# Moving some row gathers of a recommendation kernel from GpSimd to SyncE

## The chip, the cores and the metric

The kernel runs on one core of one Trainium2 chip. The metric is the device time in microseconds (us) of one execution. The time before is 13297.63 us, the median of three runs (13260.15 to 13308.35). The profile is of one execution, which took 13172.43 us.

## What is computed

For each of 16384 requests there are 69 item ids and one label id. Each id picks a row of 96 floats from a table of 100001 rows. A small network (attention) turns each item row, together with the label's row, into one weight; the weighted rows are summed in 10 groups of fields; and three layers on top (200, 80, 1) turn the 10 sums and the label's row into one number.

```python
u  = emb[batch_user]                     # [B, 69, 96]   B = 16384
ql = emb[batch_label[:, 0]]              # [B, 96]
q  = broadcast(ql[:, None, :], u.shape)
z  = concatenate([q, u, q - u, q * u], axis=-1)
h  = _dice(z @ W1 + b1, a1, EPS_DICE)    # 64 wide; _dice needs a sigmoid
h  = h @ W2 + b2                         # 16 wide
att = h @ W3 + b3                        # 1 wide
pre = where((batch_user < ITEM_NUM)[..., None], u * att, 0.0)
pooled = einsum('gf,bfe->bge', window, pre).reshape(B, G * E)   # G = 10 groups
x = concatenate([pooled, ql], axis=-1)
h = _dice(_bn_eval(x @ Wf1 + bf1, EPS_BN), af1, EPS_DICE)       # 200
h = _dice(_bn_eval(h @ Wf2 + bf2, EPS_BN), af2, EPS_DICE)       # 80
return h @ Wf3 + bf3                                            # 1
```

The work is thus 16384 x 70 = 1.15 million rows of 384 B, picked at random from memory, and a modest amount of matrix work in float32 on each.

## The kernel before

The requests are worked on in 32 blocks of 512. The items of a block are cut into 69 chunks of 512 rows: 64 "main" chunks of 8 requests x 64 fields, and 5 "tail" chunks with one of the last five fields of all 512 requests. Two chunks make a pair, and there are 1104 pairs. One tile of 128 rows is fetched by one gather of GpSimd (an indirect DMA with 128 ids, a list that lies in the on-chip memory): 276 gathers per block for the items, and 4 for the labels.

```python
def gather(table, dst, index):
    nc.gpsimd.indirect_dma_start(out=dst, out_offset=None, in_=table,
                                 in_offset=bass.IndirectOffsetOnAxis(ap=index, axis=0))

def head_gather(n):                       # the 4 x 128 label rows of block n
    q = bpool.tile([P, NQ, E], F32, tag="q", name=f"q{n}")       # 2 buffers
    for k in range(NQ):
        gather(emb, q[:, k, :], ids[n][:, NT + k : NT + k + 1])
    return q

def fetch(i, between=None):               # pair i: 8 gathers, 8 transpositions
    u = upool.tile([P, 8, E], F32, tag="u", name=f"u{i}")        # 14 buffers
    ...
    for j in range(2):
        ...
        n, k = chunk(2 * i + j)
        ptr = ps_tr.tile([E, 512], F32, tag="tr", name=f"ptr{i}_{j}")
        for t in range(4):
            gather(rows, u[:, 4 * j + t, :], ids[n][:, 4 * k + t : 4 * k + t + 1])
            nc.tensor.transpose(ptr[:, t * P : (t + 1) * P], u[:, 4 * j + t, :], ident)
        # VectorE: quT = ptr * q; ScalarE: uT = copy of ptr
        ...
```

After the transposition a pair goes through these steps, each some pairs later: `hidden` (the first layer on TensorE, tile ph, two steps after the fetch; ScalarE and VectorE make y of it), `attend_rows` and `spread` (the attention weight of each row, tiles prow, patt and rw), and `pool`, which multiplies the rows with their weights and sums them by group, reading u once more:

```python
def pool(i):
    u, rw = us.pop(i), rws.pop(i)
    ...
    pa = ps_acc.tile([E, 2, NS, G], F32, tag="acc", name=f"acc{i}")   # 1 buffer
    for j, n, k in todo:                  # main chunks only
        for t in range(4):
            nc.tensor.matmul(pa[:, j, 2 * t : 2 * t + 2, :]..., u[:, 4 * j + t, :], rw[:, t, j, :], ...)
    ...                                   # VectorE: pooled <- pa
```

The order of all this is a plan with one step for each pair, written out by hand. `POOL_LAG` is 8:

```python
for i in range(close):
    if i >= POOL_LAG:
        at(i, pool_of(i - POOL_LAG))
    if i >= 3 and (i - 3) % 4 == 3:
        at(i, rows_of(i - 6, 4))
    ...
    if i >= 2:
        at(i, hidden_of(i - 2))
    at(i, fetch_of(i))
...
for n in range(NBLK):
    first, end = n * NCH // 2, ((n + 1) * NCH - 1) // 2
    if n > 0:
        if n % NIDS == 1:
            at(first - 20, lambda n=n: load_ids(n))        # ids of 4 blocks, by SyncE
        at(first - 14, lambda n=n: qs.__setitem__(n, head_gather(n)))
        at(first - 11, lambda n=n: head_turn(n, qs.pop(n)))  # transposes the label rows
        at(first - 9, lambda n=n: head_rows(n))
```

At the end of the last block the top layers are done by quarters of 128 requests, in between the last pairs (`quarter[r][s]` is step s of quarter r: 0 to 3 and 4 to 7 the two halves of the first layer, 8 the second, 9 the third):

```python
d = NPAIR
at(d, pool_of(c + 4), hidden_of(c + 7), pool_of(c + 5), *quarter[2][0:4], rows_of(c + 6, 2), *quarter[2][4:8])
at(d, quarter[2][8], spread_of(c + 6, 2), quarter[2][9], quarter[3][0])
at(d, pool_of(c + 6), pool_of(c + 7), lambda: store(B // P - 1), *quarter[3][1:])
```

The weights come in two packs, `near` (first layer) by SyncE and `far` (top layers) by ScalarE's queue.

Of the kernel before, what the change touches and what calls it, by code (L numbers as in the profile page):

```python
# [32 lines left out]
F32 = mybir.dt.float32  # L33
I32 = mybir.dt.int32
# [4 lines left out]
P = 128  # L39
B, F, E, G = 16384, 69, 96, 10  # L40
ITEM_NUM = 100000
H1, H2 = 64, 16
D1, D2 = 200, 80
DH = D1 // 2

BLK = 512
NBLK = B // BLK
# [5 lines left out]
NQ = BLK // P  # L53
NT = NCH * 4
# [5 lines left out]

POOL_LAG = 8

NIDS = 4

EARLY = 20
# [49 lines left out]
def rec_kernel(  # L115
    ctx: ExitStack,
    tc: tile.TileContext,
    idx0: bass.AP,
    idx: bass.AP,
    emb: bass.AP,  # L120
    rows: bass.AP,
    near: bass.AP,
# [3 lines left out]
    nc = tc.nc  # L126
# [4 lines left out]
    tpool = ctx.enter_context(tc.tile_pool(name="tpool", bufs=4))  # L131
    ypool = ctx.enter_context(tc.tile_pool(name="ypool", bufs=6))
    rpool = ctx.enter_context(tc.tile_pool(name="rpool", bufs=2))
    bpool = ctx.enter_context(tc.tile_pool(name="bpool", bufs=2))
    xpool = ctx.enter_context(tc.tile_pool(name="xpool", bufs=1))

    def by_field(ap):

        return ap.rearrange("e (s o) -> e s o", o=1).to_broadcast([ap.shape[0], NS, FM])

    ids = {0: const.tile([P, NCOL], I32, name="ids0")}
    nc.sync.dma_start(out=ids[0], in_=idx0)

    def load_ids(n):

        t = ipool.tile([P, NIDS, NCOL], I32, tag="ids", name=f"ids{n}")
        nc.sync.dma_start(out=t.rearrange("p b n -> p (b n)"), in_=idx[(n - 1) // NIDS])
        for k in range(NIDS):
            ids[n + k] = t[:, k, :]
# [2 lines left out]
    wn = const.tile([P, NEAR.width], F32, name="wn")  # L152
    nc.sync.dma_start(out=wn, in_=near)
    wf = const.tile([P, FAR.width], F32, name="wf")
    nc.scalar.dma_start(out=wf, in_=far)

    ident = const.tile([P, P], F32, name="ident")
    make_identity(nc, ident)
# [25 lines left out]
    for i in range(2):  # L184
        t = const.tile([E + 1, BLK], F32, name=f"qT{i}")
# [55 lines left out]
    ps_h = ctx.enter_context(tc.tile_pool(name="ps_h", bufs=2, space=PSUM))  # L241
    ps_x = ctx.enter_context(tc.tile_pool(name="ps_x", bufs=2, space=PSUM))
    ps_acc = ctx.enter_context(tc.tile_pool(name="ps_acc", bufs=1, space=PSUM))
    ps_m = ctx.enter_context(tc.tile_pool(name="ps_m", bufs=1, space=PSUM))
# [11 lines left out]
    def gather(table, dst, index):  # L256
        nc.gpsimd.indirect_dma_start(  # L257
            out=dst,
            out_offset=None,
            in_=table,  # L260
            in_offset=bass.IndirectOffsetOnAxis(ap=index, axis=0),
        )
# [5 lines left out]
            k = NMAIN + k - EARLY if k < EARLY + NTAIL else k - NTAIL  # L268
        return n, k

    def head_gather(n):

        q = bpool.tile([P, NQ, E], F32, tag="q", name=f"q{n}")
        for k in range(NQ):
            gather(emb, q[:, k, :], ids[n][:, NT + k : NT + k + 1])
        return q

    def head_turn(n, q):
        pq = ps_x.tile([E, BLK], F32, tag="x", name=f"pq{n}")
        for k in range(NQ):  # L280
            nc.tensor.transpose(pq[:, k * P : (k + 1) * P], q[:, k, :], ident)
        nc.vector.tensor_copy(qTs[n % 2][0:E, 0:BLK], pq)
# [18 lines left out]
    def fetch(i, between=None):  # L301

        u = upool.tile([P, 8, E], F32, tag="u", name=f"u{i}")
        uT = []
        quT = tpool.tile([E, 2, 512], F32, tag="quT", name=f"quT{i}")
        for j in range(2):
            if j == 1 and between:
                between()
            n, k = chunk(2 * i + j)
            ptr = ps_tr.tile([E, 512], F32, tag="tr", name=f"ptr{i}_{j}")  # L310
            for t in range(4):
                gather(rows, u[:, 4 * j + t, :], ids[n][:, 4 * k + t : 4 * k + t + 1])
                nc.tensor.transpose(ptr[:, t * P : (t + 1) * P], u[:, 4 * j + t, :], ident)  # L313
            q = qTs[n % 2][0:E]
            if k < NMAIN:
                nc.vector.tensor_tensor(  # L316
                    quT[:, j, :].rearrange("e (s f) -> e s f", f=FM),
                    ptr.rearrange("e (s f) -> e s f", f=FM),
                    by_field(q[:, k * NS : (k + 1) * NS]),
                    ALU.mult,  # L320
                )
            else:
                nc.vector.tensor_tensor(quT[:, j, :], ptr, q[:, 0:BLK], ALU.mult)
            uT.append(room(k))
            nc.scalar.copy(uT[j][0:E], ptr)  # L325
        return u, uT, quT

    def hidden(i, uT, quT):

# [57 lines left out]
    def pool(i):  # L387

        u, rw = us.pop(i), rws.pop(i)
        todo = [(j, *chunk(2 * i + j)) for j in range(2)]  # L390
        todo = [(j, n, k) for j, n, k in todo if k < NMAIN]
        if not todo:
            return
        pa = ps_acc.tile([E, 2, NS, G], F32, tag="acc", name=f"acc{i}")
        for j, n, k in todo:
            for t in range(4):
                nc.tensor.matmul(  # L397
                    pa[:, j, 2 * t : 2 * t + 2, :].rearrange("e n g -> e (n g)"),
                    u[:, 4 * j + t, :],
                    rw[:, t, j, :],  # L400
                    start=True,
                    stop=True,
                )
        if len(todo) == 2:
            _, n, k = todo[0]
            nc.vector.tensor_copy(  # L406
                pooled[n][:, :, k * NS : (k + 2) * NS].rearrange("e g s -> e s g"),
                pa.rearrange("e j s g -> e (j s) g"),
            )
        else:  # L410
            j, n, k = todo[0]
            nc.vector.tensor_copy(
                pooled[n][:, :, k * NS : (k + 1) * NS].rearrange("e g s -> e s g"), pa[:, j]
            )
# [10 lines left out]
    def top1(n, cols, h, part, p1):  # L425

        if part == 0:
            p1 = ps_m.tile([DH, BLK], F32, tag="m", name=f"p1_{n}_{h}_{cols.start}")[:, cols]
        for k in range(part * KTOP // 4, (part + 1) * KTOP // 4):
            if k < NTAIL:  # L430
                w, x = V[:, k], pres[n][:, k, cols]
            elif k == NTAIL:
                w, x = wf1[:, G], qTs[n % 2][0:E, cols]
            else:
                w, x = wf1[:, k - NTAIL - 1], pooled[n][:, k - NTAIL - 1, cols]
            nc.tensor.matmul(p1, w[:, h * DH : (h + 1) * DH], x, start=(k == 0), stop=(k == KTOP - 1))  # L436
        if part < 3:
            return p1
        g1 = xpool.tile([DH, BLK], F32, tag="g1", name=f"g1_{n}_{h}_{cols.start}")[:, cols]
        dice(x1s[n][:, h, cols], g1, p1, bf1c[h], dice1[h])  # L440
# [17 lines left out]
    def store(n):  # L458

        p4 = ps_x.tile([n, P], F32, tag="x", name="p4")  # L460
        nc.tensor.transpose(p4, res[:, 0:n], ident)
        r = ypool.tile([P, 512], F32, tag="y", name="r")[0:n, 0:P]
        nc.vector.tensor_copy(r, p4)
        nc.sync.dma_start(out=out[0 : n * P].rearrange("(m p) o -> m (p o)", p=P), in_=r)
# [6 lines left out]
        nc.vector.tensor_scalar(r, p3, bf3c[0:1], None, ALU.add)  # L471
        nc.sync.dma_start(out=out[B - P :].rearrange("p o -> o p"), in_=r)

    pooled, pres, x1s, x2s, qs, us, hs, ys, bands, rws, p1s = ({} for _ in range(11))

    def top_steps(n, cols):

# [14 lines left out]
    def rows_of(b, n):  # L492
        return lambda: attend_rows(b, n)

    def spread_of(b, n):
        return lambda: spread(b, n)

    def pool_of(k):
        return lambda: pool(k)

    def hidden_of(k):
        return lambda: ys.__setitem__(k, hidden(k, *hs[k]))
# [25 lines left out]
    def at(step, *work):  # L528
        plan.setdefault(step, []).extend(work)
# [15 lines left out]
    c = close  # L545
# [9 lines left out]
    for n in range(NBLK):  # L555
        first, end = n * NCH // 2, ((n + 1) * NCH - 1) // 2
        if n > 0:
            if n % NIDS == 1:
                at(first - 20, lambda n=n: load_ids(n))
            at(first - 14, lambda n=n: qs.__setitem__(n, head_gather(n)))  # L560
            at(first - 11, lambda n=n: head_turn(n, qs.pop(n)))
            at(first - 9, lambda n=n: head_rows(n))
        if n < NBLK - 2:
            for s, work in enumerate(top_steps(n, slice(0, BLK))):
                at(end + POOL_LAG + 4 + s, work)
        elif n == NBLK - 2:
            for s, work in enumerate(top_steps(n, slice(0, BLK))):
                at(end + POOL_LAG + s // 2, work)
# [3 lines left out]
    quarter = [top_steps(NBLK - 1, slice(r * P, (r + 1) * P)) for r in range(NQ)]  # L572
# [2 lines left out]
        at(c + s // 3, quarter[1][s])  # L575

    d = NPAIR
    at(d, pool_of(c + 4), hidden_of(c + 7), pool_of(c + 5), *quarter[2][0:4], rows_of(c + 6, 2), *quarter[2][4:8])
    at(d, quarter[2][8], spread_of(c + 6, 2), quarter[2][9], quarter[3][0])
    at(d, pool_of(c + 6), pool_of(c + 7), lambda: store(B // P - 1), *quarter[3][1:])  # L580

    with tc.manual_schedule():
        qs[0] = head_gather(0)
        head_turn(0, qs.pop(0))
        head_rows(0)
        ones()
        for i in range(NPAIR + 1):
            for work in plan.pop(i, []):
                work()
# [63 lines left out]
```

## Time and profile before

| engine or queue | busy, us | share of the span | instructions |
|---|---|---|---|
| TensorE, matmuls | 8747.3 | 66% | 41797 |
| TensorE, weight loads (beside matmuls) | 4554.2 | 35% | 41797 |
| VectorE | 3029.0 | 23% | 5325 |
| ScalarE | 3167.1 | 24% | 4969 |
| GpSimd | 8455.0 | 64% | 8966 |
| DMA queue of the gathers, of 16 engines | | 16.0% | 286720 packets |

The span is 13170.6 us. How to read it: the busy time of an engine leaves out what its sequencer does between two instructions, so an engine can be full at less than 100%. TensorE's clock is granted by a throttle; its mean was 0.732 of full speed. In the tables of groups a row names the line, the engine, the operation and "tile written <- tiles read", then the count, the busy time in all, the mean of one in ns, and the idle time just before these instructions with what ended most of it. In the timeline a row has its start, its duration (both us), the engine, the line, and in square brackets the idle time before it with what ended it. "issue" means that the profile shows nothing that the engine waited for.

The gathers begin at 7.04 us and the last one starts at 13051.49 us; the last instruction ends at 13170.6 us.

### The profile page before, as it was taken

What the parts mean: (1) busy time and instruction counts of PE and PEld (TensorE: products, weight loads), DVE (VectorE), ACT (ScalarE), POOL (GpSimd) and SP (SyncE); (2) the same over time, 40 slices, a digit from 0 to 9 for tenths busy, and PEclk for the clock granted to TensorE, in tenths of its full rate; (3) what the DMA queues carried; (4) which work ended last, traced back from release to release, by engine and by line L of the source; (5) the groups of instructions that cost most, each with busy time, mean ns of one, the idle gap of its engine ahead of it and who ended that gap; (6) DMA issues with size and microseconds to landing.
All of it is one profiled execution on the core that took longest, in us unless ns stands there. A gap on an engine that the chain in (4) does not pass through costs nothing.

```text
span 13170.6 us, 108463 instructions
## 1 busy us (share of the span) xinstructions
PE 8747.3 (66%) x41797; PEld 4554.2 (35%) x41797; DVE 3029.0 (23%) x5325; ACT 3167.1 (24%) x4969; POOL 8455.0 (64%) x8966
## 2 busy tenths in 40 slices
PE   3666666667666676666766667666666666676667
PEld 2333333333333333333333333333333333333334
DVE  2222222222222222222222222222222222222222
ACT  1222222222222222222222222222222222222222
POOL 6666666666666666666666666666666666666664
PEclk6777777777777777767777777777777777777777
DMA  1111111111111111111111111111111111111111
GB/s 40 35 35 34 34 34 37 34 36 34 34 36 34 35 35 35 37 34 34 35 34 37 33 35 34 34 36 35 35 35 33 36 34 35 35 35 35 35 34 22
DMA packets 288946, 454.19 MB, mean 34 GB/s; under 512 B 143538, under 2 KB 143922, under 8 KB 288306
## 3 DMA queue, kind: packets, MB, share of 16 engines
q0 software_dynamic: 286720, 440.98, 16.0%
q8 instruction: 335, 5.49, 0.2%
q1 hardware_dynamic: 1570, 5.04, 0.1%
q14 instruction: 177, 1.45, 0.0%
q10 hardware_dynamic: 144, 1.24, 0.0%
HBM read 446.61 MB, written 0.07 MB: 34 GB/s over the span
## 4 chain that ended last, share of the span: by engine, by line
PE 54%; issue 20%; another core or an unknown queue 16%; POOL 4%; ACT 3%; DVE 3%; DMA 1%; DVEq 0%; POOLq 0%
PE acc L397 11%; PE ptr L313 9%; PE ph L338 9%; PE ph L342 8%; PE p L436 7%; PE prow L353 4%; POOL u L257 3%; PE patt L370 1%; DVE quT L316 1%; PE pa L362 1%; ACT uT L325 1%; ACT y L345 1%; PE ph L335 1%; PE pc L290 1%
## 5 line engine op out<-in xcount | busy, mean ns | idle before, releaser
L257 POOL DMA_INDIRECT u<-in_rows,ids x8832 | 8333.2, 944 | 4552.4 <-issue 2367.4
L397 PE MATMUL acc<-rw,u 128*96 128x20 f32 x16384 | 1922.1, 260 | 1844.3 <-issue 1436.2
L397 PEld LDWEIGHTS acc<-rw,u 128*96 128x96 f32 x16384 | 1911.1, 197 | 2083.9 <-issue 1613.1
L313 PE MATMUL ptr<-ident,u 128*96 128x128 f32 x8832 | 1594.5, 316 | 1395.4 <-issue 1099.1
L325 ACT COPY uT<-ptr 96x512 f32<-96x512 f32 x2208 | 1283.3, 581 | 3091.3 <-DVE quT L316 1905.9
L313 PEld LDWEIGHTS ptr<-ident,u 128*96 128x96 f32 x8832 | 1079.1, 143 | 2732.2 <-issue 2182.7
L344 ACT ACTIVATE y<-ph 128x512 f32<-128x512 f32 x1104 | 659.3, 597 | 5104.0 <-remote 2661.7
L342 PE MATMUL ph<-quT,wn 96*64 96x512 f32 x4416 | 1693.6, 744 | 165.9 <-issue 158.6
L346 DVE TENSOR_TENSOR y<-ph,y 128x512 f32<-128x512 f32 x1104 | 763.5, 692 | 4287.1 <-ACT y L345 2399.0
L338 PE MATMUL ph<-uT,A 128*64 128x512 f32 x4096 | 1631.8, 800 | 145.8 <-issue 142.8
L316 DVE TENSOR_TENSOR quT<-ptr,qT 96x512 f32<-96x512 f32 x2048 | 1337.6, 680 | 1419.3 <-remote 892.2
L406 DVE COPY pooled<-acc 96x160 f32<-96x160 f32 x1008 | 429.6, 426 | 3547.6 <-remote 2121.3
L345 ACT ACTIVATE y<-y,wn,na1c 128x512 f32<-128x512 f32 x1104 | 897.8, 813 | 36.7
L342 PEld LDWEIGHTS ph<-quT,wn 96*64 96x64 f32 x4416 | 449.0, 172 | 1201.8 <-issue 1199.3
L353 PE MATMUL prow<-y,v 128*32 128x512 f32 x2208 | 629.5, 787 | 254.1 <-issue 150.2
L436 PE MATMUL p<-pooled,wf 96*100 96x512 f32 (+1 forms) x1400 | 616.5, 583 | 0.0
L338 PEld LDWEIGHTS ph<-uT,A 128*64 128x64 f32 x4096 | 280.6, 162 | 683.7 <-issue 664.9
L355 ACT COPY row<-prow 128x512 f32<-128x512 f32 (+1 forms) x277 | 161.8, 584 | 1421.8 <-remote 878.8
L370 PE MATMUL patt<-ident,row 128*128 128x128 f32 x1108 | 241.2, 338 | 277.6 <-issue 203.7
L436 PE MATMUL p<-pre,V 96*100 96x512 f32 (+1 forms) x700 | 372.7, 665 | 40.6 <-issue 25.8
L436 PEld LDWEIGHTS p<-pooled,wf 96*100 96x100 f32 x1400 | 233.7, 179 | 291.7 <-issue 291.6
L375 DVE SCALAR_TENSOR_TENSOR rw<-patt,bb,wn 128x320 f32<-128x320 f32 x554 | 273.4, 534 | 142.2 <-remote 64.3
(66 smaller groups left out, 2139.8 us busy)
## 6 DMA issues: line engine op xcount, KB each, us to landing
u<-in_rows,ids POOLq DMA_INDIRECT x8832
ids<-in_idx SPq DMA_DIRECT2D x8, 560.0 KB
q<-in_emb,ids POOLq DMA_INDIRECT x128
wf<-in_far ACTq DMA_DIRECT2D x1, 1209.0 KB
wn<-in_near SPq DMA_DIRECT2D x1, 236.0 KB
ids<-in_idx SPq DMA_DIRECT2D x1, 140.0 KB
out<-r SPq DMA_DIRECT2D x1, 63.5 KB
out<-r SPq DMA_DIRECT2D x1, 0.5 KB
```

The costliest lines, as they stand in the source:

```text
L257: nc.gpsimd.indirect_dma_start(out=dst, out_offset=None, in_=table, in_offset=bass.IndirectOffsetOnAxis(ap=index, axis=0),)
L313: nc.tensor.transpose(ptr[:, t * P : (t + 1) * P], u[:, 4 * j + t, :], ident)
L316: nc.vector.tensor_tensor(quT[:, j, :].rearrange("e (s f) -> e s f", f=FM), ptr.rearrange("e (s f) -> e s f", f=FM), by_field(q[:, k * NS ...
L325: nc.scalar.copy(uT[j][0:E], ptr)
L338: nc.tensor.matmul(p, As[n % 2][:, k // 4, :], uT[j], start=True, stop=False)
L342: nc.tensor.matmul(p, Wp, quT[:, j, :], start=False, stop=True)
L344: nc.scalar.activation(y, ph, AF.Sigmoid, scale=S_DICE)
L345: nc.scalar.activation(y, y, AF.Identity, bias=a1c, scale=na1c)
L346: nc.vector.tensor_mul(y, ph, y)
L353: nc.tensor.matmul(pr[32 * k : 32 * (k + 1), :], v2, ys[b + k], start=True, stop=True)
L397: nc.tensor.matmul(pa[:, j, 2 * t : 2 * t + 2, :].rearrange("e n g -> e (n g)"), u[:, 4 * j + t, :], rw[:, t, j, :], start=True, stop=True,)
L436: nc.tensor.matmul(p1, w[:, h * DH : (h + 1) * DH], x, start=(k == 0), stop=(k == KTOP - 1))
```

## The change

Three things change. First, in each block but the first, the four tiles of label rows and one tile of item rows (the first of chunk 8, `SOLO = 32` counted in tiles) are no longer gathered by GpSimd. SyncE loads the 640 ids of the block (20 x 32), reads 32 of them at a time into registers, and issues one copy for each row. This is spread over 20 steps of the plan, from 32 to 13 pairs before the block. It is meant to take work off GpSimd, which issues all the gathers. Second, the pack `far` is loaded by SyncE behind the first ids and `near`, so that these need not share the DMA engines with it. Third, the work at the end of the last block is ordered anew, and in the last two quarters the second half of the first layer gets an accumulation buffer of another pool, so that less of it waits.

```diff
+NLD = 32
+PARTS = P // NLD
+SOLO = 4 * 8
...
+    spool = ctx.enter_context(tc.tile_pool(name="spool", bufs=2))
...
-    nc.scalar.dma_start(out=wf, in_=far)
+    nc.sync.dma_start(out=wf, in_=far)
...
-    def head_gather(n):
-        q = bpool.tile([P, NQ, E], F32, tag="q", name=f"q{n}")
+    def first_head():
+        q = bpool.tile([P, NQ, E], F32, tag="q", name="q0")
         for k in range(NQ):
-            gather(emb, q[:, k, :], ids[n][:, NT + k : NT + k + 1])
+            gather(emb, q[:, k, :], ids[0][:, NT + k : NT + k + 1])
         return q
+
+    def load_solo(n):
+        t = spool.tile([(NQ + 1) * PARTS, NLD], I32, tag="sid", name=f"sid{n}")
+        nc.sync.dma_start(out=t, in_=solo[n])
+        return t
+
+    def fetch_rows(table, dst, index):
+        _, at = nc.values_load_multi_w_load_instructions(
+            index, engines=[mybir.EngineType.SP], min_val=0, max_val=ITEM_NUM, ...)
+        for i, row in enumerate(at):
+            nc.sync.dma_start(out=dst[i : i + 1, :], in_=table[bass.ds(row, 1), :])
+
+    def solo_part(n, part):
+        if part == 0:
+            qs[n] = bpool.tile([P, NQ, E], F32, tag="q", name=f"q{n}")
+        if part == NQ * PARTS:
+            solos[n] = spool.tile([P, E], F32, tag="solo", name=f"solo{n}")
+        k, m = divmod(part, PARTS)
+        table, dst = (emb, qs[n][:, k, :]) if k < NQ else (rows, solos[n])
+        fetch_rows(table, dst[m * NLD : (m + 1) * NLD, :], sids[n][part : part + 1, :])
...
             for t in range(4):
-                gather(rows, u[:, 4 * j + t, :], ids[n][:, 4 * k + t : 4 * k + t + 1])
-                nc.tensor.transpose(ptr[:, t * P : (t + 1) * P], u[:, 4 * j + t, :], ident)
+                if n > 0 and 4 * k + t == SOLO:
+                    tiles.append(solos.pop(n))
+                else:
+                    tiles.append(u[:, 4 * j + t, :])
+                    gather(rows, tiles[-1], ids[n][:, 4 * k + t : 4 * k + t + 1])
+                nc.tensor.transpose(ptr[:, t * P : (t + 1) * P], tiles[-1], ident)
...
-            p1 = ps_m.tile([DH, BLK], F32, tag="m", ...)[:, cols]
+            banks, tag = (ps_h, "h") if n == NBLK - 1 and cols.start >= BLK // 2 and h == 1 else (ps_m, "m")
+            p1 = banks.tile([DH, BLK], F32, tag=tag, ...)[:, cols]
...
-            at(first - 14, lambda n=n: qs.__setitem__(n, head_gather(n)))
+            at(first - 33, lambda n=n: sids.__setitem__(n, load_solo(n)))
+            for part in range((NQ + 1) * PARTS):
+                at(first - 32 + part, lambda n=n, part=part: solo_part(n, part))
...
-    at(d, pool_of(c + 4), hidden_of(c + 7), pool_of(c + 5), *quarter[2][0:4], rows_of(c + 6, 2), *quarter[2][4:8])
-    at(d, quarter[2][8], spread_of(c + 6, 2), quarter[2][9], quarter[3][0])
-    at(d, pool_of(c + 6), pool_of(c + 7), lambda: store(B // P - 1), *quarter[3][1:])
+    at(d, pool_of(c + 4), hidden_of(c + 7), pool_of(c + 5), *quarter[2][0:4], rows_of(c + 6, 2), quarter[2][4])
+    at(d, spread_of(c + 6, 2), *quarter[2][5:8], pool_of(c + 6), quarter[2][8], pool_of(c + 7))
+    at(d, quarter[2][9], quarter[3][0], lambda: store(B // P - 1), *quarter[3][1:])
```

More of the change, by code (lines that the diff above doesn't have):

```diff
@@ L119, in rec_kernel @@
     idx: bass.AP,
+    solo: bass.AP,
     emb: bass.AP,
@@ L269, in chunk @@
         return n, k
-    def head_gather(n):
-        q = bpool.tile([P, NQ, E], F32, tag="q", name=f"q{n}")
+    def first_head():
+        q = bpool.tile([P, NQ, E], F32, tag="q", name="q0")
         for k in range(NQ):
-            gather(emb, q[:, k, :], ids[n][:, NT + k : NT + k + 1])
+            gather(emb, q[:, k, :], ids[0][:, NT + k : NT + k + 1])
         return q
+    def load_solo(n):
[4 more added lines that the diff above has]
+        _, at = nc.values_load_multi_w_load_instructions(
+            index,
+            engines=[mybir.EngineType.SP],
+            min_val=0,
+            max_val=ITEM_NUM,
+            skip_runtime_bounds_check_because="ids are rows of the table",
+        )
+        for i, row in enumerate(at):
[8 more added lines that the diff above has]
+        fetch_rows(table, dst[m * NLD : (m + 1) * NLD, :], sids[n][part : part + 1, :])
     def head_turn(n, q):
@@ L303, in fetch @@
         u = upool.tile([P, 8, E], F32, tag="u", name=f"u{i}")
-        uT = []
+        uT, tiles = [], []
         quT = tpool.tile([E, 2, 512], F32, tag="quT", name=f"quT{i}")
@@ L325, in fetch @@
             nc.scalar.copy(uT[j][0:E], ptr)
-        return u, uT, quT
+        return tiles, uT, quT
     def hidden(i, uT, quT):
@@ L398, in pool @@
                     pa[:, j, 2 * t : 2 * t + 2, :].rearrange("e n g -> e (n g)"),
-                    u[:, 4 * j + t, :],
+                    u[4 * j + t],
                     rw[:, t, j, :],
@@ L427, in top1 @@
         if part == 0:
-            p1 = ps_m.tile([DH, BLK], F32, tag="m", name=f"p1_{n}_{h}_{cols.start}")[:, cols]
+            banks, tag = (ps_h, "h") if n == NBLK - 1 and cols.start >= BLK // 2 and h == 1 else (ps_m, "m")
+            p1 = banks.tile([DH, BLK], F32, tag=tag, name=f"p1_{n}_{h}_{cols.start}")[:, cols]
         for k in range(part * KTOP // 4, (part + 1) * KTOP // 4):
@@ L472, in top3_last @@
         nc.sync.dma_start(out=out[B - P :].rearrange("p o -> o p"), in_=r)
-    pooled, pres, x1s, x2s, qs, us, hs, ys, bands, rws, p1s = ({} for _ in range(11))
+    pooled, pres, x1s, x2s, qs, us, hs, ys, bands, rws, p1s, sids, solos = ({} for _ in range(13))
     def top_steps(n, cols):
@@ L577, in rec_kernel @@
     d = NPAIR
-    at(d, pool_of(c + 4), hidden_of(c + 7), pool_of(c + 5), *quarter[2][0:4], rows_of(c + 6, 2), *quarter[2][4:8])
-    at(d, quarter[2][8], spread_of(c + 6, 2), quarter[2][9], quarter[3][0])
-    at(d, pool_of(c + 6), pool_of(c + 7), lambda: store(B // P - 1), *quarter[3][1:])
+    at(d, pool_of(c + 4), hidden_of(c + 7), pool_of(c + 5), *quarter[2][0:4], rows_of(c + 6, 2), quarter[2][4])
+    at(d, spread_of(c + 6, 2), *quarter[2][5:8], pool_of(c + 6), quarter[2][8], pool_of(c + 7))
+    at(d, quarter[2][9], quarter[3][0], lambda: store(B // P - 1), *quarter[3][1:])
     with tc.manual_schedule():
-        qs[0] = head_gather(0)
-        head_turn(0, qs.pop(0))
+        head_turn(0, first_head())
         head_rows(0)
@@ L617 @@
         "idx": groups.transpose(0, 2, 1, 3).reshape(-1, P, NIDS * NCOL),
+        "solo": np.concatenate([x["batch_label"].reshape(NBLK, BLK), main[:, :, SOLO]], axis=1).reshape(NBLK, -1, NLD),
         "emb": x["emb"],
```

## The prediction

> **What bounds the kernel now.** I read the page's first part, then its groups of instructions, the table of waits, and last the timeline of one stretch. The first part looks as if no engine were full; the group of the gathers is the largest of all:
>
> ```profile
> PE 8747.3 (66%) x41797; PEld 4554.2 (35%) x41797; DVE 3029.0 (23%) x5325; ACT 3167.1 (24%) x4969; POOL 8455.0 (64%) x8966
> ...
> L257 POOL DMA_INDIRECT u<-in_rows,ids x8832 | 8333.2, 944 | 4552.4 <-issue 2367.4
> ```
>
> One gather is 944 ns busy, and behind nearly each stands a gap of 0.30 us in which the engine waits for nothing (7751 such gaps make 2367.4 us). In the timeline gathers that follow each other start 1.248 us apart (7 of them from 6199.22 to 6207.95). With the 128 gathers of the label rows there are 8960: 8960 x 1.248 = 11,182 us in which GpSimd can do nothing else. They run from 7.0 to 13,052 us, so GpSimd stands still for 13,045 - 11,182 = 1,863 us. The table of waits says for whom:
>
> ```profile
> POOL u L257 <- issue: 2367.4, 7751, 1.5
> POOL u L257 <- remote: 978.9, 318, 7.4
> ...
> POOL u L257 <- PE acc L397: 462.2, 107, 39.8
> POOL u L257 <- PE ptr L313: 434.0, 201, 5.7
> ...
> PE ptr L313 <- DMA u<-in_rows,ids: 63.9, 66, 2.4
> ```
>
> The reader is to see two opposite sides. GpSimd waits for TensorE: a tile u is free only when the pooling matmul (acc) of its pair of chunks is done, 8 pairs after its transposition, and there are 14 buffers; so GpSimd is about 6 pairs (48 gathers) ahead when it stops. TensorE hardly waits for a gather: 63.9 us in the whole run. By these two alone TensorE is the bound, and a cheaper GpSimd would bring nothing.
>
> But TensorE is 66% busy, and its idle time is "issue", which no semaphore explains. The timeline shows what that is, here TensorE and then GpSimd in one stretch:
>
> ```profile
> 6174.88 0.30 PE L313 MATMUL ptr<-ident,u 128*96 128x128 f32 x1 [0.44 <-issue]
> 6194.28 2.11 PE L397 MATMUL acc<-rw,u 128*96 128x20 f32 x12 [19.10 <-issue]
> 6197.99 0.19 PE L397 MATMUL acc<-rw,u 128*96 128x20 f32 x1 [1.60 <-issue]
> ...
> 6206.40 0.19 PE L397 MATMUL acc<-rw,u 128*96 128x20 f32 x1 [2.62 <-issue]
> 6209.19 1.01 PE L353 MATMUL prow<-y,v 128*32 128x512 f32 x1 [2.60 <-issue]
> 6211.99 3.82 PE L353 MATMUL prow<-y,v 128*32 128x512 f32 x5 [1.79 <-issue]
> ```
>
> ```profile
> 6207.95 0.94 POOL L257 DMA_INDIRECT u<-in_rows,ids  x1 [0.30 <-issue]
> 6216.18 0.94 POOL L257 DMA_INDIRECT u<-in_rows,ids  x1 [7.29 <-PE prow L353]
> ```
>
> Matmuls that take 0.09 us elsewhere come 2.8 us apart here, for nearly 40 us, while GpSimd gathers without a stop; GpSimd starts its last gather at 6207.95, runs into full buffers, and some 3 us later TensorE is fast again. The same order stands at 6086-6090, 6109-6113 and 6041-6044. I take it that **the slow stretches of TensorE last as long as GpSimd keeps gathering**: GpSimd gathers for about two pairs (16 x 1.248 = 20 us), stops for some 3 us, and TensorE does its two pairs in the 12 us behind that stop. The pace is then GpSimd's time plus its stops, although the waits say the opposite. This is an inference from the order of events; I can't name the mechanism, and it is the weakest step here.
>
> **What the Trainium skill says.** *Perfetto Trace Analysis*, section "DMA Optimizations", says that where descriptor generation is the limit, spreading DMAs over the engines that can issue them may help: the idea of the change. Here GpSimd is full with issuing while the DMA queue's share is 16.0% of 16 engines, which agrees. *DMA: Bandwidth & Descriptors*, section "Why a DMA increments its semaphore by 16 and not by 1", says that a transfer of one partition runs on one DMA engine, the lowest. The trace agrees as to the number: the SyncE queue has 1570 packets; ten loads of 128 rows with 16 completions make 1440, and the two stores of 127 and 1 rows leave 130 = 127 + 1 + one completion each. So all rows of SyncE go through one DMA engine of 16. The same page, "Latency and other measured facts", gives a floor of about 600 ns for loading registers from a tensor, and *Runtime: NRT & Kernel Launch*, "Instruction fetch mechanics", about 200 ns a register. No run here shows either yet.
>
> **The change part by part.**
>
> 1. Removed from GpSimd: in each of 31 blocks 4 label gathers and one tile's gather, 31 x 5 = 155 gathers x 1.248 = **193 us**. If the number and length of GpSimd's stops stay, the end comes 193 us earlier (1.45%). If TensorE sets its own pace, nothing comes of it.
>
> 2. Added to SyncE: 31 x 640 = 19,840 row copies of 384 B, each with one small register instruction ahead, and 31 x 20 = 620 register loads of 32 ids. The nearest thing in the trace is the last store, of one row:
>
> ```profile
> 13168.46 0.26 SPq L472 DMA_DIRECT2D out<-r  x1
> ```
>
> 0.26 us, and I add 0.12 us for the register instruction and the gaps (issues at the start stand about 0.05 us apart beyond their own time): an estimate of 0.38 us a row, 640 x 0.38 = 243 us per block. The 20 loads are 12 us by the floor of 600 ns and 128 us by 200 ns a register, by the skill's figures. SyncE needs an estimated **255 to 371 us per block**; a block lasts 13,045 / 32 = 408 us. It fits, with 9 to 37% to spare. Rows begin 32 pairs ahead of their block and the tiles have two buffers, so a short lag is absorbed. With 70 us for loads a row may cost up to (408 - 70) / 640 = 0.53 us before SyncE becomes the bound. Each copy also waits for the one eight before it; at the 2 us or so that a gather takes from issue to landing that is 0.25 us a row, below the issue time.
>
> 3. Added to TensorE: the transpositions of label rows and of the extra tile wait for eight DMA semaphores instead of few, 31 x 16 = 496 waits of 0.05 us (a semaphore instruction of TensorE lasts 51 ns in the trace), at most 25 us, most of it in its idle time: +10 us.
>
> 4. The weights of the top layers (1209 KB) now go behind the first ids and the near weights on one queue. Before, the first ids landed at about 7.0 us with that load beside them. At most -3 us; I put -2.
>
> 5. The end: the pooling matmuls of the last two pairs come one at a time between other matmuls, and the last quarter's second half has a PSUM bank of its own. What it can take away is seen here:
>
> ```profile
> 13151.25 0.42 DVE L406 COPY pooled<-acc 96x160 f32<-96x160 f32 x1 [3.99 <-PE acc L397]
> 13151.73 2.75 PE L397 MATMUL acc<-rw,u 128*96 128x20 f32 x16 [0.52 <-DVE pooled L406]
> ```
>
> Gaps of 0.5, 1.0 and 1.4 us on TensorE and some matmuls at half clock (2.75 instead of 1.53 us): -5 us. The drain of the last six pairs, from 13,052 to 13,170 us, stays.
>
> Sum: -193 + 10 - 2 - 5 = -190, that is 13,108 us. As one of the rivals may hold in part, I put the middle at 13,130.
>
> **The rivals.** (a) *TensorE is the bound by itself.* For it: the waits above. Against: its slow stretches end with GpSimd's stops, also where these come late. Then only parts 3 to 5 remain: about 13,300 us. (b) *SyncE becomes the bound.* For it: 19,840 issues in a row, estimated from a single store whose address is fixed; a register address may cost more. At 0.65 us a row and 70 us of loads a block would take 486 us, in all some 15,000 us. It is steep: nothing up to 0.53 us, and then 20 us a block for each further 0.03 us. (c) *The rows disturb what the stops restore.* If TensorE needs a pause of all DMA traffic and not of GpSimd alone, a steady stream of rows takes the pauses away; 13,400 us or more. The traffic is little (640 rows of 35,840 per block), so I hold it for possible, not likely. (d) *The slow stretches shorten more than in proportion*, as fewer gathers fall between two stops: below 13,030.
>
> **Range and chances.** The three runs before lie within 48 us, 0.36%. I give 60% to the sum above, 15% to (a), 12% to (b), 8% to (c), 5% to (d). More than 2% faster is below 13,032 us: it needs (d) or a gain a third above the whole 193 us: 0.15. More than 2% slower is above 13,564: most of (b) and part of (c): 0.15. Range 12,980 to 13,400.
>
> **What would show it.** In the profile after: 8801 gathers of u (31 fewer) and 4 of q (124 fewer), still 944 ns; GpSimd's idle time for TensorE near 1,900 us (kept: step 1 right; grown by about 190: rival a). SyncE's rows about 0.4 us apart with pauses in each block, and no wait of TensorE for rows worth naming (a long wait of pq or of the extra tile's transposition for a DMA: rival b). The slow stretches still end with GpSimd's stops (if they no longer do: c). The drain after the last gather 118 us less about 5. Wrong above all if the pace isn't GpSimd's.

## The result and the profile after

The changed kernel takes **16980.15 us** (median of 4 runs, 16967.74 to 17004.23) where the kernel before takes 13295.63 us: the ratio is **1.2781**, 95% interval 1.276 to 1.2802. I had predicted 13,130 and a range of 12,980 to 13,400. The profiled execution has a span of 16978.9 us.

The first part of the page and two of its groups, in the order of the lines shown of before (engine totals; then line, engine, operation, tiles, count, busy time, mean ns, idle time before and what ended it):

```profile
PE 8996.8 (53%) x41797; PEld 4647.2 (27%) x41797; DVE 2996.8 (18%) x5325; ACT 3159.1 (19%) x4969; POOL 8330.6 (49%) x8811
...
L264 POOL DMA_INDIRECT u<-in_rows,ids x8801 | 8325.6, 946 | 8536.5 <-PE acc L436 4174.2
...
L316 PE MATMUL pq<-ident,q 128*96 128x128 f32 x128 | 44.4, 378 | 3892.9 <-DMA q<-in_emb 3868.8
```

The 8801 gathers still take 946 ns, but GpSimd is idle for 8536.5 us before them, where it was 4552.4. The last row is new: 128 small matmuls (they transpose label rows) are busy for 44.4 us and wait 3868.8 us for the DMA of q, that is, for SyncE's rows. The table of waits (waiting engine and line, releaser: us in all, times, longest) has the same chain in three steps:

```profile
POOL u L264 <- PE acc L436: 4174.2, 132, 133.0
PE pq L316 <- DMA q<-in_emb: 3868.8, 67, 73.0
DVE qT L317 <- PE pq L316: 3762.0, 32, 135.3
```

TensorE waits for label rows about twice in each of 31 blocks, and GpSimd, out of buffers, waits for TensorE. A plain reading of GpSimd's first row would blame TensorE; the second row shows that TensorE is only the messenger. **SyncE is the bound.** Is it waiting for something itself? The waits of SyncE's own queue:

```profile
SPq L301 <- DMA q<-in_emb: 179.1, 325, 1.4
SPq L301 <- DMA solo<-in_rows: 82.7, 141, 1.5
SPq L293 <- DMA sid<-in_solo: 16.4, 11, 5.1
```

These are under 300 us of 16,979 (the one longer row, left out here, is a store at the end that waits 408.5 us for its result): the wait of each copy for the one eight before it does not matter. SyncE is busy executing. What its instructions cost is in the list of the instructions that touch q (ns: shortest/median/longest):

```profile
L301 SPq MOVE q<-in_emb x15872: 1/29/1422, 9.9 to 16401.4; - x199
L301 SPq DMA_DIRECT2D q<-in_emb x15872: 1/225/1398, 10.0 to 16401.4; - x199
```

The median copy is cheap: with its address arithmetic (37 ns), the move (29 ns) and the gaps, rows follow each other every 0.408 us. But single instructions take up to 1.4 us. The timeline shows when. First two lines of SyncE (start, length of the run of rows, count), from two windows that overlap a little:

```profile
6000.27 12.70 SPq L301 DMA_DIRECT2D q<-in_emb  x7
...
6012.33 3.72 SPq L301 DMA_DIRECT2D q<-in_emb  x9
```

and GpSimd in the same stretch:

```profile
6006.98 0.95 POOL L264 DMA_INDIRECT u<-in_rows,ids  x1 [0.30 <-issue]
6008.23 0.94 POOL L264 DMA_INDIRECT u<-in_rows,ids  x1 [0.30 <-issue]
6012.94 0.95 POOL L264 DMA_INDIRECT u<-in_rows,ids  x1 [3.77 <-remote]
6014.19 0.95 POOL L264 DMA_INDIRECT u<-in_rows,ids  x1 [0.30 <-issue]
```

Seven rows in 12.7 us, most of it while GpSimd gathers; then nine rows in 3.7 us (0.41 us each), from 3.2 us after GpSimd's last gather ended at 6009.17. The whole trace has the same order: register loads left out, 92% of the rows that start 2.5 to 3 us after the start of the last gather before a stop are followed by the next row within 0.5 us, and 9% of those that start 2 to 2.5 us after it. It is the picture that the prediction showed for TensorE. In the records of the slow part SyncE's instructions, whatever they are, mostly start 0.70 or 1.40 us after the one before, or right behind it.

Summed over the records: 11,110 of the intervals between rows are under 0.5 us (4,158 us in all); 8,729 are longer (12,389 us, the 620 register loads of about 2.1 us among them). Together that is 16,547 / 31 = **534 us per block**, and 16,547 + 10 (start) + 422 (the work of the last block behind its last rows) is the span. GpSimd needs only 275 x 1.248 = 343 us a block.

### The profile page after: what moved, and what is told of

It reads as the page before. It is cut to its first block, busy times and chain, and to the rows that moved or that the text cites. A ratio compares the mean times of both kernels' runs of the same rounds, so it can differ in the third digit from the quotient of the medians.

```text
span 16978.9 us, 169158 instructions
## 1 busy us (share of the span) xinstructions
PE 8996.8 (53%) x41797; PEld 4647.2 (27%) x41797; DVE 2996.8 (18%) x5325; ACT 3159.1 (19%) x4969; POOL 8330.6 (49%) x8811
## 5 line engine op out<-in xcount | busy, mean ns | idle before, releaser
L264 POOL DMA_INDIRECT u<-in_rows,ids x8801 | 8325.6, 946 | 8536.5 <-PE acc L436 4174.2
L436 PE MATMUL acc<-rw,u 128*96 128x20 f32 x16322 | 2046.6, 268 | 1860.6 <-issue 1692.2
L436 PEld LDWEIGHTS acc<-rw,u 128*96 128x96 f32 x16322 | 2016.1, 207 | 2092.5 <-issue 1883.3
L316 PE MATMUL pq<-ident,q 128*96 128x128 f32 x128 | 44.4, 378 | 3892.9 <-DMA q<-in_emb 3868.8
L352 PE MATMUL ptr<-ident,u 128*96 128x128 f32 x8801 | 1475.8, 310 | 774.1 <-issue 471.8
L377 PE MATMUL ph<-uT,A 128*64 128x512 f32 x4096 | 1681.5, 847 | 67.0 <-issue 63.1
L392 PE MATMUL prow<-y,v 128*32 128x512 f32 x2208 | 755.5, 894 | 414.7 <-issue 258.5
```

Of the source, the lines that this page charges most:

```text
L352: nc.tensor.transpose(ptr[:, t * P : (t + 1) * P], tiles[-1], ident)
L377: nc.tensor.matmul(p, As[n % 2][:, k // 4, :], uT[j], start=True, stop=False)
L392: nc.tensor.matmul(pr[32 * k : 32 * (k + 1), :], v2, ys[b + k], start=True, stop=True)
L436: nc.tensor.matmul(pa[:, j, 2 * t : 2 * t + 2, :].rearrange("e n g -> e (n g)"), u[4 * j + t], rw[:, t, j, :], start=True, stop=True,)
```

## The experiments

**Theory 1**: the rows are slow because of the stretches, in which SyncE as well as TensorE is slowed while GpSimd gathers; without them a row is 0.41 us and SyncE fits. **Theory 2** (rival): a row with a register address costs that much by itself, by its own issue, its waits or its DMA engine. **Theory 3** (rival): the rows disturb the gathers or TensorE.

The runs came in five groups, each on a chip of its own (B to F), and this turned out to matter as much as the edits. The chip of the result is A; whether it is one of D, E and F is not known. Each group was also run at one time, so what is called a difference between chips below could be one between times; within a group from B to F the kernel before stays within 0.25%. The kernels without gathers (e2, e3, e10, e11), e12, e14 and e16 were timed once each.

| chip | runs | kernel before, us | slow stretches |
|---|---|---|---|
| A | the result | 13295.63 | yes |
| B | e1 to e4 | 11269.88 | no |
| C | e5 to e8 | 11253.10 | no |
| D | e9 to e12 | 13283.63 | yes |
| E | e13 to e16 | 13196.68 | yes |
| F | e17, e18 | 13204.35 | yes |

On B and C the unchanged kernel is 15% faster and purely bound by GpSimd: 8960 x 1.248 = 11,182 us, and the rest is start and end. No trace of it was kept there; in that of e1, the nearest to it, no two gathers on B start more than 1.41 us apart. Every ratio below is against the kernel before on the same chip.

### Without the rows (chip B)

Only the second and third part of the change:

```diff
-    nc.scalar.dma_start(out=wf, in_=far)
+    nc.sync.dma_start(out=wf, in_=far)
     ...and the new order and buffer at the end of the last block
```

> The kernel before with the second and third part of the change alone (weights behind the ids, new order at the end), no rows by SyncE. Theory 1 (the rows of SyncE are the whole loss): about 13,288 us, 7 us less than before, within 0.3%. Theory 2 (some of the loss comes from the other two parts): above 13,500 us.

Measured: 11253.06 us, ratio 0.9986 (0.998 to 0.9993), that is 17 us less. The two small parts bring a little here, 8 to 23 us by the interval. This chip shows no loss at all, so that they don't cause it elsewhere rests on the trace of A, where the wait is for rows, and on the 256-row kernel on D below, which contains both and is 159 us slower, not 3,700.

### Without gathers, without and with rows (chip B)

In both, GpSimd fetches item rows only for the first 14 pairs; later pairs reuse those tiles, so the output isn't the reference's.

```diff
+        u = kept[i % 14] if i >= 14 else upool.tile(...)
...
-                gather(rows, ...)
+                if i < 14:
+                    gather(rows, ...)
```

> The kernel before, but the item rows are gathered for the first 14 pairs only and these 14 tiles are used again for all later pairs; the arithmetic of all 1104 pairs stays, and the label gathers. Theory 1 (TensorE's slow stretches come from GpSimd's gathers running on without a pause): no slow stretches, about 6.2 us a pair, 7,000 us (up to 8,000 us). Rival (TensorE is the bound by itself, by its clock or its own pace): the slow stretches stay and the time is above 12,500 us.

> The changed kernel with item rows gathered for the first 14 pairs only; SyncE still issues its 640 rows per block. Theory 1 (rows take 0.41 us each, and 1.4 us only while GpSimd gathers): rows 0.41 us apart everywhere, 640 x 0.41 + 20 x 2.1 = 304 us per block, SyncE is then the bound of a run of about 9,500 us. Rival (rows are slow by themselves): still some 530 us per block, above 16,000 us.

The kernel before without gathers takes 6462.12 us:

```profile
PE 6304.2 (98%) x41797; PEld 3649.2 (56%) x41797; DVE 2927.8 (45%) x5325; ACT 3159.8 (49%) x4969; POOL 229.5 (4%) x246
```

TensorE at 98% is what "TensorE is the bound" would look like; its own need is about half of the kernel's time. The granted clock was 0.989 in this run and 0.732 in the kernel before on A: if all of TensorE's work took longer in that proportion, it would need an estimated 6,460 x 0.989 / 0.732 = 8,730 us, still far below 13,296. The changed kernel without gathers takes 10012.78 us, 500 more than I expected, and is bound by SyncE:

```profile
PE pq L316 <- DMA q<-in_emb: 3431.7, 61, 62.7
```

Its rows stand 0.408 us apart throughout (median) and a load of 32 registers takes 2.15 us: 640 x 0.408 + 20 x 2.15 = 304 us a block. The trace has 313, with the wait for the block's ids and some longer gaps: the rows run from 12 to 9,704 us. The 307 us behind the last row are the last block's work, which I had forgotten. Theory 2 is weakened: a row costs 0.408 us, not 0.77.

### Stops of GpSimd, first try (chip B)

```diff
                 gather(rows, u[:, 4 * j + t, :], ...)
+                if (8 * i + 4 * j + t) % 8 == 7:
+                    nc.gpsimd.tensor_copy(still, u[:, 4 * j + t, :][0:1, 0:1])
```

GpSimd reads one value of the tile just gathered and so waits until it has landed.

> The kernel before, and behind each 8 gathers GpSimd copies one element of the tile just gathered, so that it waits until that gather has landed before it issues the next. Theory 1a (the slow stretches need gathers in flight without a break, and a break of about 1 us ends them): TensorE keeps its fast pace, a pair takes 10.0 us + 1.1 to 1.3 us, 12,250 to 12,450 us, and GpSimd's stops for TensorE nearly vanish. Theory 1b (a stop must be longer, about 3 us): the stops stay and the breaks come on top, 13,300 to 14,500 us. Rival (TensorE sets the pace by itself): GpSimd only waits less for TensorE, 13,300 us.

Measured: 13616.03 us, ratio 1.2083 (1.2063 to 1.2103). On a chip without stretches the stops are pure cost, about 2.1 us each beyond a plain step: (13,616 - 11,270) / 1104. I had put 1.1 to 1.3 us.

### The changed kernel again, and other numbers of rows (chip C)

The 256-row version lets SyncE fetch two label tiles per block and leaves the rest to GpSimd; the 768-row version adds a second item tile. In the last one all gathers stay, and 640 rows per block go into tiles that nothing reads.

```diff
-            for part in range((NQ + 1) * PARTS):
+            for part in range(2 * PARTS):            # 256 rows
...
+            for part in range((NQ + 2) * PARTS):     # 768 rows
...
-        table, dst = (emb, qs[n][:, k, :]) if k < NQ else (rows, solos[n])
+        table, dst = (emb, spare[n][:, k % 2, :]) if k < NQ else (rows, solos[n])   # unread
```

> The changed kernel itself once more, beside the kernel before on one chip. In the experiments so far the kernel before took 11,270 us and no engine showed the stretches with 0.7 us and more between instructions. Theory 1 (rows are 0.41 us apart where these stretches are absent, and SyncE is the bound only through them): if they are absent here, 11,270 - 193 - 17 = 11,060 us, 2% faster; if they are there, 16,980 us. Rival (rows are slow beside gathers in any case): 16,000 us or more, even where the kernel before takes 11,270.

> The changed kernel with 256 rows per block by SyncE (two tiles of labels); the other two label tiles and the item tile stay with GpSimd. Theory 1: without the slow stretches 11,250 - 62 x 1.248 = 11,173 us; with them SyncE needs 256 x 0.8 = 205 us of a block's 408 and the time is 13,290 - 77 = 13,210 us. Rival (rows disturb in proportion to their number): a loss of 0.4 of that of 640 rows.

> The changed kernel with one more item tile per block by SyncE, 768 rows. Theory 1 without slow stretches: SyncE needs 768 x 0.408 + 24 x 2.15 = 365 us per block, GpSimd 274 gathers x 1.248 = 342 us; SyncE becomes the bound, 31 x 365 + 150 = 11,450 us, slower than with 640 rows by some 400 us. Rival (SyncE still has room): 31 x 1.248 = 39 us less than with 640 rows. With slow stretches: above 19,500 us.

> GpSimd does all 8960 gathers as before, and SyncE issues the 640 rows per block as well, into tiles that nobody reads. It leaves nothing out; it shows what the rows do beside the gathers when nothing waits for them. Theory 1 without slow stretches: as e1, within 0.5% (11,250 us), GpSimd's 1.248 us a gather unchanged. Rival (rows take DMA or sequencer time from gathers or TensorE): above 11,400 us. With slow stretches: the end is set by SyncE's last row, 16,000 to 25,000 us.

| rows per block | us | ratio | 95% interval |
|---|---|---|---|
| 640, the changed kernel | 11049.70 | 0.9821 | 0.9805 to 0.9837 |
| 256 | 11164.43 | 0.9920 | 0.9903 to 0.9936 |
| 768 | 11968.11 | 1.0640 | 1.0622 to 1.0658 |
| 640, unread, all gathers kept | 11241.58 | 0.9990 | 0.9982 to 0.9999 |

**The same kernel that loses 28% on chip A wins 1.8% on chip C.** The list of instructions on q, in the changed kernel on C:

```profile
L301 SPq MOVE q<-in_emb x15872: 29/29/29, 10.4 to 10114.8; - x199
L301 SPq DMA_DIRECT2D q<-in_emb x15872: 224/225/305, 10.5 to 10114.9; - x199
```

The medians are those of chip A, 29 and 225 ns; the tail up to 1.4 us is gone. As GpSimd gathers beside these rows without a stop, a row isn't dear by itself: theory 2 is false. GpSimd's idle time is the gap of 0.30 us behind each gather and hardly more:

```profile
L264 POOL DMA_INDIRECT u<-in_rows,ids x8801 | 8306.4, 944 | 2684.0 <-issue 2401.6
```

And SyncE's queue waits for buffers, as it runs ahead (the store at the end is again left out):

```profile
SPq L301 <- PE pq L316: 468.0, 16, 35.6
SPq L293 <- DMA sid<-in_solo: 40.7, 30, 5.6
```

With 768 rows the margin is used up: the rows run from 10 to 11,644 us, 375 us a block against GpSimd's 342, and the wait for rows is back:

```profile
PE pq L316 <- DMA q<-in_emb: 2536.0, 66, 62.8
```

I missed by 500 us there: 10 us a block, which make 320, and the last block, 317 us behind the last row where I had put 150. The unread rows leave the gathers and TensorE alone, so theory 3 is false on this chip.

### The same questions on a chip with the stretches (chip D)

The edits are those above: 256 rows, the two kernels without gathers, and stops after 8.

> The kernel with 256 rows per block by SyncE in place of 640. If this chip shows the stretches of 0.70 us per instruction (the kernel before then takes about 13,300): SyncE needs 256 x 0.77 + 8 x 2.2 to 8 x 4 = 215 to 229 us of a block of about 420 us, so it isn't the bound, and the time is 13,150 to 13,300; if SyncE's rows were slowed for another reason than a lack of time per block, it would be over 13,800. If the chip doesn't show them (kernel before about 11,260): 11,165, as in the run before.

> The kernel before with only the first 14 pairs' gathers; the tiles are reused. If the gathers cause the stretches, TensorE runs freely on any chip: 6,460. If the stretches belong to the chip and not to the gathers: over 9,000 on a chip whose kernel before takes 13,300.

> The changed kernel with its rows and without the gathers after the first pairs. If the gathers cause the stretches, rows stay at 0.408 us on any chip: 10,010. If the stretches come without the gathers too, rows take about 0.77 us on a chip whose kernel before takes 13,300, and the time is 16,000 or more.

> The kernel before, with GpSimd waiting after each 8 gathers until the last of them has landed. On a chip with the stretches: if a stop of GpSimd of some 3 us frees TensorE for the next 13 us, TensorE's wait falls and the time is 13,300 to 13,700, set by the pauses; if the stretches go on regardless, over 14,500. On a chip without them: 13,616, as in the run before.

| kernel on D | us | same kernel on B or C |
|---|---|---|
| before | 13283.63 | 11269.88 |
| before without gathers | 6550.06 | 6462.12 |
| changed, without gathers | 10144.26 | 10012.78 |
| before, stop after each 8 gathers | 13602.88 | 13616.03 |
| 256 rows, ratio 1.0118 (1.0089 to 1.0148) | 13442.39 | 11164.43 |

With gathers, rows are slow on D too. In the 256-row kernel 2,818 of the 7,935 intervals between rows are under 0.5 us, where the same kernel on C has 7,507, and the tail up to 1.4 us is there:

```profile
L301 SPq DMA_DIRECT2D q<-in_emb x7936: 1/225/1413, 9.9 to 12316.7; - x199
```

Without gathers, TensorE and SyncE run as on B, but for 1.3%: 18,730 of the rows of the changed kernel come under 0.5 us after the last, where it was 11,110 on A. **So the stretches need the gathers**, on a chip that has them. The stops bring the two chips together as well. The first part of the page of the kernel with stops, on D:

```profile
PE 10160.4 (75%) x41797; PEld 5048.8 (37%) x41797; DVE 3120.7 (23%) x5325; ACT 3180.6 (23%) x4969; POOL 8681.6 (64%) x10070
```

and on B:

```profile
PE 10159.7 (75%) x41797; PEld 5057.9 (37%) x41797; DVE 3126.6 (23%) x5325; ACT 3192.7 (23%) x4969; POOL 8697.0 (64%) x10070
```

The two lines agree within 0.4%. The stops cost 2,350 us on B and 320 on D, where they also take TensorE's stretches away.

The 256 rows missed: I expected at most 13,300. SyncE has ample time there (no wait of pq for rows worth naming), GpSimd has 62 gathers less to issue, and yet it is 159 us slower. So theory 3 may hold in part on this chip; the two small parts, which the kernel contains, were not run alone on it.

### How long may GpSimd gather? (chips E and F)

Stops after 12, 16 and 24 gathers in the kernel before, and stops in the changed kernel and in the 256-row version; the edit is that of the first stops with another number.

> The kernel before, with GpSimd waiting after each 16 gathers until the last has landed. A stop costs 2.17 us more than a plain step (measured with stops after 8). With no stretches in streaks of 16 gathers (20 us): 8960 x 1.248 + 552 x 2.17 = 12,380, on any chip. If on a chip with the stretches (kernel before about 13,290) TensorE falls behind within 16 gathers: 12,700 to 13,300.

> The same with a stop after each 24 gathers: 8960 x 1.248 + 368 x 2.17 = 11,980 without stretches. On a chip with them: TensorE needs 17.6 us for three pairs and, by the traces before, has about 13 us free after a stop, so it falls behind and the time is 12,500 to 13,300.

> The changed kernel with a stop after each 16 gathers. Without stretches: 8805 x 1.248 + 550 x 2.17 = 12,180. If on a chip with them SyncE is free for 13 of 22 us and else at 1.44 us a row, a row takes 0.58 us on average, a block 426 us, and SyncE is the bound: 31 x 426 + 450 = 13,650. If the stops keep the stretches away from SyncE too: 12,180. Without any effect of the stops: 17,000.

> 256 rows per block by SyncE and a stop after each 16 gathers: SyncE has time to spare in any case, so 8898 x 1.248 + 554 x 2.17 = 12,310 on any chip, if streaks of 16 gathers leave TensorE enough.

> The changed kernel with a stop of GpSimd after each 8 gathers. If the slow rows come from the stretches alone and such stops keep them away: GpSimd is the bound, 8805 x 1.248 + 1100 x 2.17 = 13,375 on any chip. If SyncE's rows stay slow on a chip with the stretches (kernel before 13,200 to 13,300): 16,000 to 17,000.

> The kernel before with a stop after each 12 gathers: 8960 x 1.248 + 746 x 2.17 = 12,800 without stretches, on any chip. If they begin within streaks of 12 gathers on a chip that has them: about 13,150, as with stops after 16.

| kernel (chip) | us | ratio, 95% interval |
|---|---|---|
| before, stop after 12 (F) | 13115.26 | 0.9929 (0.9906 to 0.9951) |
| before, stop after 16 (E) | 13157.98 | 0.9969 (0.9953 to 0.9985) |
| before, stop after 24 (E) | 13225.24 | one run, kernel before 13196.68 |
| changed, stop after 8 (F) | 14594.56 | 1.1057 (1.0992 to 1.1123) |
| changed, stop after 16 (E) | 16843.48 | 1.2757 (1.2703 to 1.2811) |
| 256 rows, stop after 16 (E) | 13353.38 | one run, kernel before 13196.68 |

Stops after 12 or more bring next to nothing: after 12 the time is 315 us above the 12,800 without stretches, so these begin within a dozen gathers. The 256 rows with stops after 16 missed my 12,310 by 1,040 us. In the changed kernel the stops after 8 take back some 2,390 us (16,980 on A, 14,595 on F: two chips, the ratios are 1.28 and 1.11), stops after 16 nothing to speak of. I had expected 13,375 for stops after 8; that would have made GpSimd the bound, but the chain is still SyncE's:

```profile
PE pq L316 <- DMA q<-in_emb: 2903.3, 55, 73.2
```

The traces tell why. Counted from the records from 600 us on, while GpSimd gathers: how many instructions an engine starts per us (SyncE: rows; TensorE: weight loads and semaphore instructions), by the time since the first gather behind a stop of GpSimd (two gathers over 1.9 us apart).

| us since the gathers resumed | rows, changed (A) | rows, changed, stop after 8 (F) | TensorE, before (A) | TensorE, before, stop after 8 (D) | the same (B) |
|---|---|---|---|---|---|
| 0 to 2.5 | 1.73 | 1.95 | 4.6 | 5.02 | 5.01 |
| 2.5 to 5 | 0.91 | 1.27 | 4.9 | 3.38 | 3.42 |
| 5 to 7.5 | 0.88 | 1.03 | 4.8 | 2.91 | 2.89 |
| 7.5 to 10 | 0.56 | 0.63 | 6.1 | 1.75 | 1.76 |
| 10 to 12.5 | 0.51 | | 4.1 | | |
| 12.5 to 15 | 0.39 | | 2.5 | | |
| 15 to 17.5 | 0.37 | | 1.2 | | |
| 17.5 to 20 | 0.28 | | 0.75 | | |

Undisturbed, SyncE does 1 / 0.408 = 2.45 rows per us, and 2.05 with its register loads and waits for ids in between (19,840 rows in 9,692 us without gathers on B). On A it is below that from the first 2.5 us of a run of gathers and sinks to a seventh. TensorE holds out for some 10 us and then falls to a sixth. In the two last columns TensorE falls as it runs out of gathered tiles, alike on both chips: within 8 gathers no slowing shows. That is why stops after 8 free TensorE and only partly SyncE. Theory 1 stands for the loss on A, with the correction that the slowing is gradual and sets in at different times on the two engines.

No version beat both kernels on every chip. Where there are no stretches the changed kernel is the best of those run; where there are, the kernel before with stops after 12 gathers gains 0.7%, and I did not run it on B or C; on B stops after 8 cost 21%.

## Why the prediction was wrong, point by point

- **Where the gain would come from (part 1)**: 193 us for 155 gathers. On C the change brings 203 us, of which 17 are the small parts by the run on B; the remaining 186 are 4% under the sum. The step was right for a kernel whose pace is GpSimd's. On A it could not show, as SyncE set the pace; and with 256 rows on D and E the fewer gathers brought nothing (+159 us; and 13,353 against 13,158 with stops after 16). "If the number and length of GpSimd's stops stay" was the condition, and it didn't hold: with stops after 16 GpSimd stopped 763 times with 256 rows, 680 times without rows (from 600 us on).
- **What SyncE needs (part 2): the step that failed.** "It fits, with 9 to 37% to spare" rested on 0.38 us a row, whatever GpSimd does meanwhile. On A the mean row, loads apart, is (16,547 - 620 x 2.1) / 19,840 = 0.77 us, so SyncE needs 534 us for a block that I had given 408, and sets the pace. Undisturbed a row is 0.408 us and a load 2.15 us, and a block takes 313 us, inside my 255 to 371. For a load the Trainium skill's two figures (*DMA: Bandwidth & Descriptors*, "Latency and other measured facts", and *Runtime: NRT & Kernel Launch*, "Instruction fetch mechanics") had spanned 0.6 to 6.4 us; it is 67 ns a register here, and that replaces the 200 ns. I took the row's cost from a store at 13,168 us, 117 us behind the last gather, and from issues at the start; both stand where nothing disturbs. In the same text I showed TensorE slowed for 40 us at a time and didn't ask whether SyncE's sequencer would be. The limit of 0.53 us that I worked out was the right one to hold the row against.
- **Rival (b)** came true with 12%. Its estimate of 0.65 us a row and 15,000 us was of the right kind, its reason was not: the register address doesn't make a row dear.
- **The weakest step, "the slow stretches of TensorE last as long as GpSimd keeps gathering"**, holds on the chips that have them: no stretch without gathers (D), none within 8 gathers (D), and a rate that sinks the longer the gathers go on (A). What I missed is that it belongs to some chips and not to others.
- **Rival (a)** is false: TensorE needs 6,460 to 6,550 us by itself. **Rival (c)**: false on C (0.999 with unread rows), perhaps true in part on D. **Rival (d)** was never seen.
- **Parts 3 to 5**: the semaphore waits of TensorE were not measured alone. The weights and the end brought 17 us on B, I had 7. On A the first gather starts at 3.3 us instead of 7.0, a little more than the 3 us that I had allowed at most.

**What stays open**: why SyncE and TensorE are slowed in steps of 0.70 us while gathers run, and why on some chips and not on others. The records show no wait for it, and the transfers are hardly slower: in the changed kernel a packet of the gathers takes 117 ns on A and 108 on C (mean), a packet of the larger of the two queues that bring instructions 1,057 and 1,078. Nor is it separated whether the gathers slow the others by being issued or by their traffic, nor whether chip or time makes the difference. Also open is why 256 rows slow the kernel on D and E. There TensorE falls sooner: 7.5 to 10 us after the gathers resumed it starts 4.1 instructions per us on D with 256 rows, where the kernel before on A has 6.1.

## What to carry to other kernels

Before moving work to an idle engine, take the cost of its instructions from a stretch in which the rest of the kernel runs, not from the quiet start or end; if another sequencer is slowed there, budget the new one as slowed too. A long wait for a busy engine may be one link only: follow the table of waits until an engine turns up that waits for nothing. And a change with a slim margin should be timed on more than one chip: here the same edit was worth -1.8% and +28%.

## What the hardware showed unexpectedly

- The unchanged kernel takes 11,253 and 11,270 us in two of the groups, each on its own chip, and 13,197 to 13,296 us in the others.
- On the slow ones, SyncE's and TensorE's instructions often come in steps of 0.70 or 1.40 us once GpSimd has gathered for a while: from the first few us on SyncE, after about 10 us on TensorE. Of TensorE's 5,734 intervals over 0.6 us in the kernel before on A, 2,973 are within 0.06 us of one of these two; of 5,634 in the kernel without rows on B, 477.
- A one-row copy by SyncE with a register address: 37 + 29 + 225 ns and gaps, 0.408 us a row. 32 registers from on-chip memory: 2.15 us.
- A stop until a gather has landed costs GpSimd 2.1 us beyond the plain step of 1.248 us.
